# Two of four token tiles first: the first batch's hand-over from the second linear to the shared expert, split into halves

## The chip, the cores and the metric

The kernel runs on one core of a Trainium2 chip. The metric is device time in microseconds (us) of one execution. A profile records one execution, instruction by instruction; engines are named PE (TensorE), PEld (its weight loads), DVE (VectorE), ACT (ScalarE), POOL (GpSimd) and SP (SyncE).

## The reference

A gated cross-attention-like block on x of 4 batches x 512 tokens x 512 features, float32:

```python
# per batch b; smooth_quant_linear quantises tokens and weights to 8-bit steps after smoothing both per column
h = smooth_quant_linear(layernorm(x[b]), w_in[b])          # 512 -> 512
a = silu(h[:, :256]) * h[:, 256:]
x[b] += tanh(g_xattn) * smooth_quant_linear(a, w_ctx[b])   # the second linear, 256 -> 512
y = layernorm(x)                                           # all 2048 tokens
scores = softmax(y @ gate_w.T); top 2 of 16 experts, 256 places each
routed = sum over the two of weight * (silu(y @ wg[e]) * (y @ wu[e])) @ wd[e]
shared = (silu(y @ ws_gate) * (y @ ws_up)) @ ws_down       # inner size 704
out = x + tanh(g_ffn) * (routed + shared)
```

## The kernel before, in words

A batch is four tiles of 128 tokens on the partitions. For each batch, `first(b)` is the first linear (statistics, absolute maxima per column, smoothing, rounding, product) and `second(b)` the second one. For batch 0 the end of `second` is: `product(t)` (PE product into a bank of `ps_c`, then the DVE scale, L732), `residual(t)` (X += o, L739, on POOL unless told otherwise), `stats(t)` (DVE, L292 and L293), `norm` (one over the standard deviation of all four tiles, three steps of `inv_std`: L275, a square root on ACT at L266, then small DVE instructions L279 to L286), `normal(t)` (y, L753) and `turn_y(t)` (four PE transposes, L773, and an ACT copy, L354, into `xT`, features on partitions, tokens in columns).

The shared expert reads `xT`. `glu_steps` makes one chunk of 128 inner features: a gate product `pg` and an up product `pu` (L972), each four products over the features with 512 token columns (an f32 product is two passes, so it shows as two MATMULs), `silu` (L976) on ACT and `times` (L979) on DVE into `hT`. There are five full chunks, a rest of 64 features (`pr`), and then the products of tokens with ws_down (`sh`, L1037). These products are what PE fills its time with while the other engines work on the quantised linears of later batches.

Three things set the order on the engines. The **opening** (`Program`, L1250 to L1323) is an order written out by hand for batch 0 and the start of batch 1: `opening.at(time, steps)` sorts by time, the times being keys of the order alone. Its last block, `beside`, mixes products of shared chunk 0 with batch 1's maxima (`f1.greater`, `f1.turn_max`, `wide1`), smoothing, and its scaling of tokens (`divide`, DVE) and weights (`multiply`, POOL). `idle` and `idle_x` (L1266) are transposes whose results nobody reads. After the opening, a **Plan** (L1326) orders everything up to the routed experts by estimated durations, from given times at which each engine comes free; PE steps get a margin after what they need, and shared products (rank 1e6) fill the rest. From then on every engine runs its instructions in that order, each waiting for its semaphores. Last come the 16 **routed experts** (`gather`, `gate_up` L1154, `down` L987) and batch 3's shared products with the gathering of the results (`yk`, L1699).

PSUM is held in `ps_t` (tag tp, two banks), `ps_c` (tag c, two) and `ps_mm` (tag mm, four). `chain_ps` is the pair tp and c, `beside_ps` gives banks of `ps_mm`; `columns` (L299) takes the first of a pair for its transposes, `row_broadcast` (L307) the second.

## Time and profile before

| what | us |
|---|---|
| median of the three runs | 586.7 |
| lowest and highest | 576.94, 592.93 |
| the profiled execution | 580.96 |
| its span, first to last instruction | 579.0 |
| PE busy in the span | 538.2 |
| DVE busy | 406.4 |
| ACT, POOL busy | 228.0, 140.8 |

The profile gives, for each group or instruction, the start and duration in us, the line of the kernel, the operation, out<-in by the program's names with partitions x elements, and the count; in square brackets is how long the engine had stood idle before it and what ended that. A busy engine here means that an instruction was in flight; matmuls overlap, so PE's busy time is read together with the distances between starts. The granted clock is the share of full speed that TensorE was given.

### The profile page before, as it was taken

To read this page: it belongs to the slowest core of one execution; us is meant where nothing else is said; L and a number is where in the kernel's file an instruction comes from. 1 tells how busy PE (TensorE), PEld (TensorE's weight loads), DVE (VectorE), ACT (ScalarE), POOL (GpSimd) and SP (SyncE) were. 2 spreads that over 40 slices of the span, in tenths; PEclk is the share of its full clock that TensorE was granted. 3 is DMA by queue.
4 is the path that set the end of the run, shared out by engine and by line. 5 is a ranking of instruction groups with operands and counts; after the bars stand their busy time and mean duration, and the time that the engine had idled before them with its cause. 6 is when DMAs were issued, how large, how long until landed. Compare 5 with 4: busy or idle time off the path is not lost.

```text
span 579.0 us, 5971 instructions
## 1 busy us (share of the span) xinstructions
PE 538.2 (93%) x1830; PEld 283.9 (49%) x1830; DVE 406.4 (70%) x927; ACT 228.0 (39%) x379; POOL 140.8 (24%) x155
## 2 busy tenths in 40 slices
PE   0667799999999999999989999999999999999977
PEld 0544444544444444544455555555555555644422
DVE  6889788999998997985478666665755665315445
ACT  4554577538516353140146254444443444211000
POOL 1315032253261511201321022111111100027740
PEclk9978999999999999999999999999999999999989
DMA  8971012013205092010787999999999995336864
GB/s 283 366 243 37 1 73 72 1 44 82 57 1 109 15 326 68 2 72 3 169 253 219 219 284 282 250 269 271 291 241 261 287 259 144 86 101 199 247 216 164
DMA packets 93967, 95.07 MB, mean 164 GB/s; under 512 B 51552, under 2 KB 70240, under 8 KB 93936
## 3 DMA queue, kind: packets, MB, share of 16 engines
q1 hardware_dynamic: 84064, 69.39, 45.1%
q0 software_dynamic: 5120, 16.78, 9.2%
q10 hardware_dynamic: 4752, 8.52, 3.9%
q8 instruction: 15, 0.25, 0.2%
q14 instruction: 16, 0.13, 0.1%
HBM read 66.36 MB, written 16.78 MB: 144 GB/s over the span
## 4 chain that ended last, share of the span: by engine, by line
PE 75%; DVE 12%; issue 5%; POOL 3%; ACT 1%; DMA 1%; another core or an unknown queue 1%; SPq 0%; DVEq 0%; POOLq 0%
PE b L1154 22%; PE eo L987 14%; PE pg L972 9%; PE sh L1037 9%; PE pu L972 8%; POOL yk L1699 2%; PE pr L1011 2%; PE tp_h L1174 2%; PE acc L576 2%; DVE X L1710 1%; PE rowb L307 1%; PE sh L1043 1%; DVE scx L331 1%; PE acc L726 1%
## 5 line engine op out<-in xcount | busy, mean ns | idle before, releaser
L987 PE MATMUL eo<-wd,ehT 128*128 128x512 f32 (+1 forms) x192 | 85.1, 592 | 0.0
L1105 POOL DMA_INDIRECT xg<-xn_dram,slot_token x32 | 35.7, 1117 | 195.4 <-DMA xp<-xg 160.6
L1037 PE MATMUL sh<-wsd,hT 128*128 128x512 f32 x160 | 75.3, 607 | 4.0 <-DVE hT L979 4.0
L972 PE MATMUL pg<-xT,wsg 128*128 128x512 f32 x160 | 74.9, 597 | 0.7 <-ACT xT L354 0.7
L972 PE MATMUL pu<-xT,wsu 128*128 128x512 f32 x160 | 74.0, 595 | 0.0
L987 PEld LDWEIGHTS eo<-wd,ehT 128*128 128x128 f32 (+1 forms) x192 | 36.4, 190 | 41.6 <-issue 37.0
L354 ACT COPY xgT<-xp 128x1024 int16<-128x1024 int16 x31 | 39.5, 1339 | 27.6 <-DMA xp<-xg 27.6
L1203 DVE TENSOR_TENSOR p<-p,b 128x352 f32<-128x352 f32 x16 | 8.3, 520 | 57.6 <-PE b L1154 57.6
L1037 PEld LDWEIGHTS sh<-wsd,hT 128*128 128x128 f32 x160 | 29.5, 194 | 36.2 <-issue 30.5
L1699 POOL DMA_INDIRECT yk<-eo_dram,slot x32 | 32.6, 1020 | 51.5 <-PE pg L972 42.1
L972 PEld LDWEIGHTS pu<-xT,wsu 128*128 128x128 f32 x160 | 29.2, 190 | 30.8 <-issue 30.6
L972 PEld LDWEIGHTS pg<-xT,wsg 128*128 128x128 f32 x160 | 28.7, 190 | 31.0 <-issue 29.5
L1154 PE MATMUL b<-T,S 128*128 128x352 f32 x128 | 40.6, 460 | 0.7 <-DVE S L1145 0.7
L1154 PE MATMUL b<-wg,xgT 128*128 128x352 f32 x128 | 40.6, 460 | 0.0
L1154 PE MATMUL b<-wu,S 128*128 128x352 f32 x128 | 40.5, 459 | 0.0
L1165 ACT COPY eo_sb<-eo 128x512 f32<-128x512 f32 x32 | 18.7, 585 | 47.4 <-PE eo L987 39.4
L979 DVE TENSOR_TENSOR hT<-g,pu 128x512 f32<-128x512 f32 x20 | 13.6, 682 | 32.1 <-PE pu L972 15.6
L1154 PEld LDWEIGHTS b<-T,S 128*128 128x128 f32 x128 | 24.2, 190 | 14.5 <-issue 1.2
L1154 PEld LDWEIGHTS b<-wu,S 128*128 128x128 f32 x128 | 24.3, 190 | 13.5
L499 POOL TENSOR_TENSOR wi<-wi,s_row 128x512 f32<-128x512 f32 x16 | 19.9, 1272 | 42.5 <-ACT s_row L484 42.5
L1154 PEld LDWEIGHTS b<-wg,xgT 128*128 128x128 f32 x128 | 23.1, 190 | 10.9 <-issue 0.8
L1710 DVE SCALAR_TENSOR_TENSOR X<-yk,wk,X 128x512 f32<-128x512 f32 x32 | 23.4, 751 | 7.0 <-DMA yk<-eo_dram,slot 6.5
(235 smaller groups left out, 866.0 us busy)
## 6 DMA issues: line engine op xcount, KB each, us to landing
wg<-in_L_ffn_w_gate_dram SPq DMA_DIRECT2D x16, 704.0 KB, 7.7
wu<-in_L_ffn_w_up_dram SPq DMA_DIRECT2D x16, 704.0 KB, 6.3
wd<-in_L_ffn_w_down_dram SPq DMA_DIRECT2D x16, 512.0 KB
eo_dram<-eo_sb ACTq DMA_DIRECT2D x32, 256.0 KB, 2.0
X<-in_x_dram SPq DMA_DIRECT2D x16, 256.0 KB, 6.5
xn_dram<-yp SPq DMA_DIRECT2D x16, 256.0 KB, 2.0
out_dram<-X SPq DMA_DIRECT2D x15, 256.0 KB, 2.0
wi<-in_fside_BxS2xS_dram SPq DMA_DIRECT2D x3, 1024.0 KB
```

The lines of the kernel that those rows point to most:

```text
L354: return (vec.tensor_copy if on is vec else act.copy)(dst, src)
L499: on.tensor_tensor(w.wi[:, t, :], w.wi[:, t, :], v.s_row, ALU.mult)
L576: pe.matmul(accs[t], lhsT=block(b, w.xqT, k, t), rhs=block(b, w.wqT, k), start=(k == 0), stop=(k == HC - 1))
L972: pe.matmul(v.ps[name], lhsT=w[:, k, o : o + P], rhs=xT[:, k, :], start=(k == 0), stop=(k == HC - 1))
L979: vec.tensor_tensor(dst, v.g, v.ps["pu"], ALU.mult)
L987: pe.matmul(acc, lhsT=hT[:m, c, bass.ts(t, P)], rhs=wd[:m, c, :], start=(c == 0), stop=(c == len(chunks) - 1))
L1037: pe.matmul(accs[t], lhsT=s.hT[:, c, bass.ts(t, P)], rhs=wsd[:, c, :], start=(c == 0), stop=(c == last))
L1105: pool.indirect_dma_start(out=xg.rearrange("p l n -> p (l n)"), out_offset=None, in_=xn_dram, in_offset=bass.IndirectOffsetOnAxis(ap=slot_ ...
L1154: pe.matmul(ps[:, :I], lhsT=lhs[:, k, :], rhs=rhs[:, k, :], start=(first and k == 0), stop=(k == HALF - 1), skip_group_check=not first,)
L1165: act.copy(eo, R[e].acc[h])
L1699: pool.indirect_dma_start(out=yk, out_offset=None, in_=eo_dram, in_offset=bass.IndirectOffsetOnAxis(ap=slot[i % 2][:, tiles[i // 2] : tile ...
L1710: vec.scalar_tensor_tensor(X[:, j, :], yks[added[0]], wk[k][:, j : j + 1], X[:, j, :], ALU.mult, ALU.add)
```

## The change

The normalisation of batch 0 after the second linear, its transposes and the first shared products are split. Tiles 0 and 1 get their own inverse deviations (`norms[0]`), are normalised and transposed first; tiles 2 and 3 follow (`norms[1]`). Shared chunks 0 and 1 move into the opening together, and each of their products is issued in two halves of 256 token columns: three groups of first halves stand before the transposes of tiles 2 and 3, the fourth behind. residual(1) goes from POOL to DVE, scale(3) is issued apart from its product, and most idle transposes of that stretch are left out. `f1.turn_max` and batch 1's weight maxima take their bank from `ps_c`, as the four banks of `ps_mm` are held by the two chunks. In `beside`, both silus stand ahead of `row_s`, and both `times` at the end. The Plan starts with later times for PE, DVE, ACT and POOL and with shared chunks 2 to 4 of batch 0.

```diff
@@ -267,25 +267,30 @@
         else:
             pool.tensor_tensor(dst, src, power[:, : src.shape[1]], ALU.pow)
-    def inv_std(w, h, table=False):
+    def inv_std(w, h, table=False, ts=slice(0, TT)):
+        part = ts != slice(0, TT)
         def begin():
-            w.ve, w.r = small(TT, "ve" + h), small(TT, "r" + h)
-            vec.tensor_scalar(w.ve, w.mv[:, :, 1], LN_EPS, None, ALU.add)
+            if ts.start == 0:
+                w.ve, w.r = small(TT, "ve" + h), small(TT, "r" + h)
+            vec.tensor_scalar(w.ve[:, ts], w.mv[:, ts, 1], LN_EPS, None, ALU.add)
         def end():
+            r, ve = w.r[:, ts], w.ve[:, ts]
             if table:
-                vec.reciprocal(w.r, w.r)
-            c = small(TT, "c" + h)
-            vec.tensor_tensor(c, w.r, w.r, ALU.mult)
-            vec.scalar_tensor_tensor(c, c, -0.5, w.ve, ALU.mult, ALU.mult)
-            vec.scalar_tensor_tensor(w.r, c, 1.5, w.r, ALU.add, ALU.mult)
-            w.nmr = small(TT, "nmr" + h)
-            vec.scalar_tensor_tensor(w.nmr, w.mv[:, :, 0], -1.0, w.r, ALU.mult, ALU.mult)
-        return [begin, lambda: root(w.r, w.ve, neg_half, table), end]
+                vec.reciprocal(r, r)
+            c = small(TT, "c" + h)[:, ts]
+            vec.tensor_tensor(c, r, r, ALU.mult)
+            vec.scalar_tensor_tensor(c, c, -0.5, ve, ALU.mult, ALU.mult)
+            vec.scalar_tensor_tensor(r, c, 1.5, r, ALU.add, ALU.mult)
+            if not part:
+                w.nmr = small(TT, "nmr" + h)
+                vec.scalar_tensor_tensor(w.nmr, w.mv[:, :, 0], -1.0, w.r, ALU.mult, ALU.mult)
+        return [begin, lambda: root(w.r[:, ts], w.ve[:, ts], neg_half, table), end]
     def row_stats(mv, t, src, h):
         st = stat.tile([P, 6], F32, tag="bn" + h, name="bn" + h)
@@ -466,7 +471,7 @@
                 greater(t)
         def turn_max():
-            v.tp = columns(beside_ps if b == 1 else ps, v.am, HC)
+            v.tp = columns((ps[1],) if b == 1 else ps, v.am, HC)
         def column_max():
             v.ax = small(HC, "colx1")
@@ -805,6 +810,7 @@
         v.__dict__.update({k: f for k, f in locals().items() if callable(f)})
         v.smooth = smoothing(v, nk, "2", table=b == 0)
         v.norm = inv_std(v, "2", table=b == 0)
+        v.norms = [inv_std(v, "2", True, slice(2 * u, 2 * u + 2)) for u in range(TT // 2)]
         return v
@@ -960,16 +966,18 @@
             vec.tensor_tensor(wk[k], wk[k], den, ALU.mult)
-    def glu_steps(xT, o, dst, home):
+    def glu_steps(xT, o, dst, home, in_halves=False):
         pl, bufs = home
         v = SimpleNamespace(ps={})
-        def product(name, w, k):
-            if k == 0:
+        def product(name, w, k, ts=slice(0, S)):
+            if k == 0 and ts.start == 0:
                 v.ps[name] = ps_mm.tile([P, H], F32, tag="mm", name=name)
-            pe.matmul(v.ps[name], lhsT=w[:, k, o : o + P], rhs=xT[:, k, :], start=(k == 0), stop=(k == HC - 1))
+            pe.matmul(
+                v.ps[name][:, ts], lhsT=w[:, k, o : o + P], rhs=xT[:, k, ts], start=(k == 0), stop=(k == HC - 1)
+            )
         def silu():
             v.g = pl.tile([P, S], F32, tag="g", name="g", bufs=bufs)
@@ -978,6 +986,12 @@
         def times():
             vec.tensor_tensor(dst, v.g, v.ps["pu"], ALU.mult)
+        if in_halves:
+            halves = [slice(0, S // 2), slice(S // 2, S)]
+            gate = [[lambda k=k, ts=ts: product("pg", wsg, k, ts) for k in range(HC)] for ts in halves]
+            up = [[lambda k=k, ts=ts: product("pu", wsu, k, ts) for k in range(HC)] for ts in halves]
+            return gate, silu, up, times
         gate = [lambda k=k: product("pg", wsg, k) for k in range(HC)]
         up = [lambda k=k: product("pu", wsu, k) for k in range(HC)]
         return gate, silu, up, times
@@ -991,10 +1005,10 @@
     def shared(b, done=None):
         s = SimpleNamespace()
-        def chunk_steps(c, home=(shp, 2)):
+        def chunk_steps(c, home=(shp, 2), in_halves=False):
             if c == 0:
                 s.hT = shp.tile([P, len(CHUNKS_IS), S], F32, tag="hT", name="hT")
-            return glu_steps(xTs[b], c * P, s.hT[:, c, :], home)
+            return glu_steps(xTs[b], c * P, s.hT[:, c, :], home, in_halves)
         def chunk(c):
             gate, silu, up, times = chunk_steps(c)
@@ -1249,7 +1263,7 @@
     opening = Program()
     f0, (wide0, narrow0) = first(0), weights(0)
-    f1, (wide1, narrow1) = first(1), weights(1, beside_ps)
+    f1, (wide1, narrow1) = first(1), weights(1, (chain_ps[1],))
     s0 = second(0)
     def table(function):
         act.activation(small(1, "warm"), ones[:, :1], function)
@@ -1298,24 +1312,26 @@
     opening.at(46.7, *each(s0.steps_a), *each(s0.turn_a_tile), lambda: s0.take_a(act))
     opening.at(49.0, *each(s0.steps_w, vec), *each(s0.turn_w_tile), *f1.norm[:2], lambda: s0.take_w(vec), s0.row_ws)
     opening.at(51.2, f1.norm[2], *each(f1.absolute), lambda: s0.product(0), lambda: s0.product(1), lambda: s0.residual(0))
-    opening.at(53.5, lambda: s0.product(2), lambda: s0.residual(1), lambda: s0.stats(0), lambda: s0.product(3))
-    opening.at(55.0, lambda: s0.residual(3, vec), lambda: s0.residual(2), lambda: s0.stats(1), lambda: s0.stats(3))
-    opening.at(55.1, *each(idle_x, ts=[1, 2, 3]))
-    opening.at(58.0, lambda: s0.stats(2), s0.norm[0], *each(lambda t: idle(s0.mv[:, t, 0:1]), ts=[1, 3]), lambda: idle(s0.mv[:, 2, 0:1], 3), s0.norm[1], s0.norm[2], lambda: idle(s0.ve[:, :1], 3))
-    for t in range(TT):
-        opening.at(61.0 + 0.5 * t, lambda t=t: s0.normal(t, vec), lambda t=t: s0.turn_y(t))
+    opening.at(52.5, lambda: s0.residual(1, vec), lambda: idle_x(1), lambda: s0.stats(1), lambda: s0.stats(0), lambda: idle_x(0))
+    early, late = s0.norms
+    opening.at(55.0, early[0], early[1], lambda: s0.product(2), lambda: idle(s0.mv[:, 0, 0:1]), lambda: s0.residual(2), lambda: s0.multiplied(3), early[2])
+    for t in (0, 1):
+        opening.at(56.0, lambda t=t: s0.normal(t, vec), lambda t=t: s0.turn_y(t))
+    opening.at(57.0, lambda: s0.scale(3), lambda: s0.residual(3, vec), lambda: s0.stats(2), lambda: s0.stats(3), *late)
     sh0 = shared(0)
-    opening.at(64.0, *each(f1.greater, ts=[1, 2, 3]), *each(wide1.absolute), *each(wide1.greater, ts=[1, 2, 3]))
     def beside():
-        gate, silu, up, times = sh0.chunk_steps(0)
-        order = gate[:1] + [f1.turn_max] + gate[1:3] + [f1.column_max] + gate[3:] + [wide1.turn, wide1.end]
-        order += f1.smooth + [lambda: table(AF.Silu), silu]
-        order += up[:2] + [f1.row_rs, f1.row_s, *each(f1.multiply), *each(f1.divide)] + up[2:] + [times]
+        (gate0, silu0, up0, times0), (gate1, silu1, up1, times1) = (sh0.chunk_steps(c, in_halves=True) for c in range(2))
+        turns = [step for t in (2, 3) for step in (lambda t=t: s0.normal(t, vec), lambda t=t: s0.turn_y(t))]
+        order = gate0[0] + up0[0] + gate1[0] + turns + up1[0]
+        order += [*each(f1.greater, ts=[1, 2, 3]), f1.turn_max, *each(wide1.absolute), *each(wide1.greater, ts=[1, 2, 3])]
+        order += gate0[1] + [f1.column_max] + up0[1] + [wide1.turn, wide1.end] + gate1[1] + f1.smooth
+        order += [lambda: table(AF.Silu), silu0, silu1] + up1[1][:2] + [f1.row_rs, f1.row_s, *each(f1.multiply), *each(f1.divide)]
+        order += up1[1][2:] + [times0, times1]
         for step in order:
             step()
     opening.at(65.0, beside, lambda: s0.keep_normal(TT - 1), lambda: s0.store_normal(TT - 1))
     with tc.manual_schedule():
@@ -1324,7 +1340,7 @@
     plan = Plan(
-        dict(PE=74.5, DVE=76.5, ACT=74.0, POOL=78.0, SP=70.0, DMA=70.0, XBAR=70.0),
+        dict(PE=76.5, DVE=78.0, ACT=75.5, POOL=79.0, SP=70.0, DMA=70.0, XBAR=70.0),
         dict(tp=2, c=2, mm=4, h=3, ab=3, y=3, q=2, q2=2, aba=2, amx=1, amw=1, g=2, xT=2),
     )
     SHARED, ROUTE = 1e6, 1e5
@@ -1582,7 +1598,7 @@
     home0 = plan.add("ACT", 0.0, nothing, rank=-2.0, takes="xT")
     for t in range(TT - 1):
         plan_keep(s0, t, plan.add("ACT", 0.0, nothing, rank=-2.0, takes="y"), rank=KEEP)
-    plan_shared(0, sh0, [], range(1, FULL), home0)
+    plan_shared(0, sh0, [], range(2, FULL), home0)
     plan.margin = 3.0
     plan_scores(0, s0, [None] * TT)
     firsts, seconds = {0: SimpleNamespace(wi=None)}, {0: SimpleNamespace(wc=None)}
```

## The prediction, made before the changed kernel was run

> **What bounds the kernel now.** I read the page first, then the chain of waits, then the timelines of 48 to 90 us, where the change acts, and of 195 to 300 us, where its effect has to arrive.
>
> ```profile
> PE 538.2 (93%) x1830; PEld 283.9 (49%) x1830; DVE 406.4 (70%) x927; ACT 228.0 (39%) x379; POOL 140.8 (24%) x155
> ```
>
> TensorE is the bound: in windows of 10 us PE is busy throughout from 80 to 280 us, but for two holes of 0.7, and the chain gives it 75% of the span. The stretch where it is not full of real work is the head. PE's own timeline there:
>
> ```profile
> 53.98 0.66 PE L1266 MATMUL idle<-ident,X 128*128 128x128 f32 x4 [1.34 <-POOL X L739]
> 55.21 1.22 PE L1266 MATMUL idle<-ident,X 128*128 128x128 f32 x8 [0.58 <-POOL X L739]
> 56.58 2.61 PE L1266 MATMUL idle<-ident,mv 128*128 128x128 f32 x11
> 58.99 0.83 PE L1266 MATMUL idle<-ident,ve 128*128 128x128 f32 x3
> ...
> 63.22 1.12 PE L972 MATMUL pg<-xT,wsg 128*128 128x512 f32 x2 [0.68 <-ACT xT L354]
> ...
> 71.46 0.65 PE L307 MATMUL rowb<-ident,rs 128*128 128x128 f32 x4 [1.95 <-DVE rs L325]
> ...
> 75.19 3.27 PE L972 MATMUL pg<-xT,wsg 128*128 128x512 f32 x7
> ```
>
> The "idle" products are filler; real products begin at 63.22, behind the copy of the last tokens into xT, and PE waits once more, 1.95 us, for rs. From 75.19 on it never runs out. So whatever real work is done before 75 is saved at the end, as long as the other engines' chain keeps up. That chain is DVE's; its row that matters for the change is an add beside POOL's:
>
> ```profile
> 54.30 1.40 DVE L739 TENSOR_TENSOR X<-X,o 128x512 f32<-128x512 f32 x1
> ```
>
> **Part 1: the first half's path (earlier).** Durations are starts to starts in DVE's timeline: scale 0.72, statistics of one tile 0.80, a 4-wide instruction 0.20, a normal 0.46. Scale of tile 1 ends at 52.0. residual(1) moves from POOL to DVE and starts while POOL adds tile 0 (51.41 to 52.69). The row above is the nearest: a DVE add beside a POOL add took 1.40 and ended 0.55 after POOL's; alone such an instruction takes 0.69 (L461). So it ends at 53.25 (52.7 if nothing is shared; I take the first, the same pair of operations). Then stats(1), stats(0): 54.85; ve 55.2; scale(2) 0.75 covers the square root on ACT (0.20): 56.0; four small instructions: 56.8; normals 0 and 1 end at 57.4 and 57.9. Before, a tile took 0.6 in PE's transposes and 0.56 in ACT's copy; two tiles are in xT at 59.3. The first product starts at **59.4 instead of 63.2**.
>
> **Part 2: the second half's path (later).** Behind the early normals DVE has scale(3) 0.72, residual(3) 0.70, stats(2) and (3) 1.6, ve and root 0.6, four small ones 0.8, two normals 0.9: y of tile 3 at 63.3 instead of 61.38. The 1.9 us are the add taken from POOL (0.7), its wait for POOL (0.55) and the net four small instructions (0.8; five more, nmr gone), less waits that vanish. Queued behind them on DVE is f1.greater, batch 1's chain.
>
> **Part 3: half products.** 8 of 512 columns become 16 of 256 for each chunk. No 256-column fp32 row exists, but the neighbours agree on a price per column: 0.429 us a pass at 512 (L972), 0.296 at 352 (L1154), 0.109 at 128 (transposes): 0.84 ns. So a half product (two passes) is 0.43, its two halves cost what the whole cost. Each adds two weight loads: 32 for both chunks. *TensorE: Matmul & The Clock Gate* in the Trainium skill (Part 3, What overlaps and what doesn't) says that a weight load overlaps running matmuls only where the row groups differ, which these full-height products never do (its Part 2 also knows a background buffer that would allow it), and (LDWEIGHTS) prices a load at 128/1.2 = 107 ns: an estimate of 3.4 us more, nearly the whole gain. The rows speak otherwise: passes follow each other at 0.429 with a 0.19 us load each, and even transposes at 0.109 with a 0.14 us load. I take nothing; 3.4 stays as the bad end, below nothing is excluded as no work is left out.
>
> **Part 4: PE from 59.4.** In its order: 12 halves 5.15, transposes of tiles 2 and 3 0.87, 4 halves 1.72, turn_max 0.44, 8 halves 3.43, wide1.turn 0.44 (from 71.0), 4 halves 1.72, 2 halves 0.86: at 74.0 it stands before row_rs. y of tiles 2 and 3 (62.8, 63.3) are ready when PE comes to them at 64.5. The copies of xT end at 66.3, before the second-half products at 67.5.
> Row_rs needs rs: before, the reduce of wide1.end started 0.64 after the transposes and rs came 3.57 later; from 71.0 that is 75.2. PE waits 1.2. Then rowb 0.87 and 2 halves: **77.0**, with the score 78.0. Before, the score ran from 74.19, and it and chunk 1 would have ended at 75.19 + 6.86 = 82.05. **PE leads by 4.1 us.**
>
> **Part 5: the clock.** Filler is cut from 26 transposes to 12, so PE is nearly empty between 56.1 and 59.4 except for two transposed tiles (1.1 us).
>
> ```profile
> 52.85:56.27 3.42, 1.72 (x12) 1.00 0.00 0
> 56.27:59.68 3.41, 3.27 (x16) 0.50 0.00 0
> 59.68:63.10 3.42, 2.40 (x17) 1.00 0.00 0
> ...
> 69.90:73.30 3.40, 1.84 (x11) 1.00 0.00 0
> ```
>
> The columns are length, PE busy (instructions), granted clock, DMA share and GB/s; the cuts are the clock's own steps. A stretch with 1.72 of 3.42 us busy was followed by one at half clock; one with 1.84 was not. The same Trainium skill page (Why this matters for your kernels) warns only of gaps over some 3 us; after the change the gaps are 1.4 and 0.8 us, so by the rule nothing is lost and the lead is 4.1. By the rows, the new stretch from 56.27 has 1.4 us busy, under both, and the next 3.4 us, all half products, would run at half clock: 1.7 us lost, lead 2.4. The page (Part 1) also has the window free-running, so it need not fall there again; idle time enough lies inside for about half of its positions. I book 0.9, with ends 0 and 1.7.
>
> **Part 6: what comes late instead.** Wide1's maxima on ACT wait behind take_normal(2, 3), in one queue: from 63.06 to 66.2. Row_rs is 3.7 late; divides run from 75.9 (before 72.14). silu(0), silu(1) stand ahead of take_s on ACT, behind the 1.28 us table load: take_s 76.65 (72.58), POOL's multiplies end at 82.3 (78.2). times(0), times(1) stand ahead of max_x: 79.9.
>
> ```profile
> 75.38 2.28 DVE L331 TENSOR_REDUCE scx<-xn 128x4 f32<-128x2048 f32 x1
> 79.14 0.42 DVE L430 TENSOR_REDUCE rawc<-tp_am 128x2 f32<-128x256 f32 x1 [1.49 <-PE tp_am L299]
> ```
>
> So max_x is 4.5 late, but before there was a hole of 1.49 us behind it; scale_x is some 3 late. POOL's lateness is covered by that (max_w began at 81.64, 3.4 after the multiplies). The xn stores go to ACT and SP about 4 later; their readers, the gathers, start at 272.9. The c banks for turn_max and wide1.turn are free again before row_rs. The plan is told +1.5 for DVE and ACT, +2 for PE with one chunk less: it expects less lateness than I find, so a PE instruction of batch 1 will stand about 1 us waiting in order. I charge **1.0** (0 to 3).
>
> Is 3 us of lateness covered later? Batch 1's xT is complete at 135.2 while shared products last to 142.8; batch 2's at 206.9, to 218.0. At the end:
>
> ```profile
> 271.87 0.19 DVE L944 TENSOR_TENSOR slot_token<-slot_sum,st 128x32 int32<-128x32 f32 x1 [1.17 <-PE st L930]
> ...
> 280.85 1.33 ACT L354 COPY xgT<-xp 128x1024 int16<-128x1024 int16 x1 [16.76 <-DMA xp<-xg]
> ...
> 283.61 2.63 PE L1154 MATMUL b<-wg,xgT 128*128 128x352 f32 x8
> ```
>
> The first expert's tokens are ready at 282.2, 1.4 us before PE takes them. And in the last routing DVE stands waiting for PE's order four times (1.5 for tp_l, 0.5 for pu, 2.2 for pr through g_rest, 1.17 for st): 5.4 that shrink when PE is ahead. 3 late less 5.4 lets xgT come up to 2.4 earlier than before, about PE's lead. So it is covered.
>
> **The sum.** -4.1 + 0.9 + 1.0 = -2.2, say **-2 us**. The profiled execution took 580.96 (span 579.0 and 2.0 around it): 579. That execution is 5.7 below the median of the three runs; the middle of all four executions known is 583.8, so I forecast **582**.
>
> **Rivals.**
> - *The lead is given back.* PE stands in batch 1's chain until it is no longer ahead. For it: DVE is 80 to 95% busy from 80 to 250 us, so lateness is hardly made up. Against: 7.6 and 11 us of shared products remain behind each xT. Change 0: 584.
> - *Slower: batch 1's chain becomes the bound.* Place: take_s and max_x behind the silus and times. Price: 4.5 us at max_x, 6.2 with half clock. If the late order keeps DVE's waits for PE, it all reaches xgT, and the first expert starts 6.2 - 1.4 = 4.8 late: 588.5. It decides from the point where xgT is more than 1.4 later than 282.2. The plan that is off by 3 speaks for it; the four waits above against.
> - *It doesn't do what it says.* The head of the plan's block is already seen running inside the opening (batch 1's 128x256 maxima at 67.83, ahead of the root at 70.17), so order isn't only as written; were the first half's products to wait for all tiles (66.3), PE would have no lead: about +3, 587.
>
> **Chances.** -2 (from -5 to 0): 0.55; given back: 0.22; chain bound: 0.15; doesn't do it: 0.08. The runs of before spread over 576.9 to 592.9, 7 below and 9 above the middle, so 2% (11.7 us) is about what a measurement can tell from no change. Only the slow cases with a high draw pass +11.7, only the forecast with a low draw -11.7: 0.07 faster, 0.81 same, 0.12 slower. Range: 582 less 3 for the good end and 7 for the draw, 588 with 7, which also holds the weight loads' bad end (582 + 3.4): 572 to 595.
>
> **What would show it.** Right: the first L972 near 59.4 and at 0.215 a pass; an add of 1.2 to 1.4 on DVE at 52; rs near 75; max_x near 80; first b<-wg,xgT 1 to 4 us before 283.6. Wrong: passes over 0.25 (loads not hidden); PE waits of over 3 us in total between 80 and 280; xgT after 283.6.

## The result and the profile after

Slower. In six runs the changed kernel took 598.3 us (median; 592.7 to 605.3), the kernel before beside it 577.1: ratio 1.0351, 95% interval 1.0287 to 1.0414. The forecast was 582, no difference over 2%. The same kernel, measured again on two later occasions, took 587.8 against 576.0 (ratio 1.0198, 1.0171 to 1.0226) and 589.4 against 575.9 (1.0222, 1.0196 to 1.0249). In some sets of runs, that of the result among them, executions of either kernel are up to some 20 us longer by a wait in the last shared products, in others none is (the kernel before took 574.4 to 594.5 us in one set, 574.5 to 577.5 in another). So 12 to 13.5 us are the change's, and the other 8 to 9 of the 21 are put down to that wait.

The profiled execution took 599.9 us, span 597.7. The engine line of its page:

```profile
PE 542.2 (91%) x1844; PEld 292.6 (49%) x1848; DVE 410.0 (69%) x932; ACT 227.3 (38%) x380; POOL 139.5 (23%) x154
```

PE has 4 us more busy time and the span 18.7 more. PE's timeline where the change acts (start, duration, what, and in brackets the idle time before and what ended it):

```profile
53.22 1.80 PE L1280 MATMUL idle<-ident,X 128*128 128x128 f32 x8 [2.48 <-DVE X L744]
...
59.05 1.11 PE L778 MATMUL tp_x<-ident,y 128*128 128x128 f32 x8 [1.76 <-DVE y L758]
60.87 3.78 PE L978 MATMUL pg<-xT,wsg 128*128 128x256 f32 x8 [0.71 <-ACT xT L359]
64.45 3.21 PE L978 MATMUL pu<-xT,wsu 128*128 128x256 f32 x8
67.49 1.89 PE L978 MATMUL pg<-xT,wsg 128*128 128x256 f32 x8
69.22 1.04 PE L778 MATMUL tp_x<-ident,y 128*128 128x128 f32 x8
...
80.07 0.62 PE L312 MATMUL rowb<-ident,rs 128*128 128x128 f32 x4 [1.16 <-DVE rs L330]
...
81.92 1.06 PE L791 MATMUL logit<-xT,gateT 128*32 128x512 f32 x8
```

Real products begin at 60.87, 2.35 us earlier than before but 1.5 later than forecast. Eight half passes take 1.73 us at full clock (67.49 to 69.22), and the first eight 3.58. The transposes of tiles 2 and 3 have to wait for three such groups: 69.22, where the prediction had 64.5 for them. The score starts at 81.92 (74.19 before) and ends at 82.92. At that point PE has done the score and chunks 0 and 1, for which the prediction counted 82.05 in the kernel before: PE leaves the opening 0.9 us behind, not 4.1 ahead. The granted clock, cut at its own steps (length, PE busy, PEld, DVE, ACT, POOL, clock, DMA share, GB/s):

```profile
53.44:56.86 3.42, 3.42 (x15) 2.64 (x14) 2.48 (x8) 0.31 (x2) 0.12 (x1) 0.50 0.00 0
56.86:60.28 3.42, 1.54 (x10) 0.84 (x8) 3.28 (x7) 0.53 (x2) 1.15 (x1) 1.00 0.00 0
60.28:63.69 3.41, 2.82 (x7) 2.29 (x8) 2.92 (x10) 0.74 (x3) 0.00 (x0) 0.50 0.00 0
63.69:67.10 3.41, 3.41 (x10) 2.70 (x9) 2.99 (x5) 0.00 (x0) 0.00 (x0) 0.50 0.00 0
```

After the window with 1.54 us of PE work two windows run at half clock, not one. How many do differs between executions. In the profile of e_again the windows fall elsewhere: one from 58.58 to 61.98 holds 1.55 us of work, and only the one behind it runs at half clock. The first three groups of half products took 8.35 us here, 6.97 there and 7.71 in e_again2, against 5.19 at full clock. DVE's timeline:

```profile
51.95 1.21 DVE L744 TENSOR_TENSOR X<-X,o 128x512 f32<-128x512 f32 x1
...
55.91 0.75 DVE L737 SCALAR_TENSOR_TENSOR o<-acc,scx,ws_row 128x512 f32<-128x512 f32 x1 [0.81 <-PE acc L731]
...
56.77 1.25 DVE L286 TENSOR_TENSOR c<-r 128x2 f32<-128x2 f32 x1
...
72.01 2.28 DVE L422 TENSOR_TENSOR amw_w<-amw_w,ab_w 128x512 f32<-128x512 f32 x3 [5.24 <-ACT ab_w L418]
...
84.56 2.28 DVE L336 TENSOR_REDUCE scx<-xn 128x4 f32<-128x2048 f32 x1
```

DVE idles 5.24 us for the absolutes of wide1, which on ACT stand behind the copies of tiles 2 and 3; max_x, at 75.38 before, starts at 84.56. And the end, to be read against the lines of before (271.87 and 283.61):

```profile
284.49 0.19 DVE L950 TENSOR_TENSOR slot_token<-slot_sum,st 128x32 int32<-128x32 f32 x1 [1.78 <-PE st L936]
...
294.85 4.76 PE L1168 MATMUL b<-wg,xgT 128*128 128x352 f32 x8 [7.52 <-issue]
```

The 9.2 us of max_x have become 12.6 at the routing. PE runs out of shared products and stands 7.5 us, then starts the experts at half clock. Earlier its work came in another order: the second addition of batch 0's shared result (L1064) came at 138.7 instead of 143.7, but the first transposes of batch 1's y at 138.6 instead of 129.0, and between 140 and 160 PE was busy only 17.2 of 20 us (19.7 before). PE had done shared work early and stood later, when the chain was not ready. This is the order's doing and no lead of the opening: with the same opening and the order of before (e_order, below) that addition comes at 152.9.

Last, PE in the tail, where the result's execution stood (first two lines) and the first repetition, e_again, did not (third line):

```profile
562.42 2.74 PE L1051 MATMUL sh<-wsd,hT 128*128 128x512 f32 x6
574.18 6.99 PE L1051 MATMUL sh<-wsd,hT 128*128 128x512 f32 x10 [9.02 <-DVE hT L987]
```

```profile
563.31 7.03 PE L1051 MATMUL sh<-wsd,hT 128*128 128x512 f32 x16
```

### The profile page after: what moved, and what is told of

Same layout as the page of the kernel before. It is cut to its first block, busy times and chain, and to the rows that moved or that the text cites. A ratio compares the mean times of both kernels' runs of the same rounds, so it can differ in the third digit from the quotient of the medians.

```text
span 597.7 us, 6002 instructions
## 1 busy us (share of the span) xinstructions
PE 542.2 (91%) x1844; PEld 292.6 (49%) x1848; DVE 410.0 (69%) x932; ACT 227.3 (38%) x380; POOL 139.5 (23%) x154
## 4 chain that ended last, share of the span: by engine, by line
PE 81%; DVE 7%; DMA 6%; issue 2%; another core or an unknown queue 2%; SPq 1%; ACT 1%; POOL 0%; DVEq 0%
PE b L1168 22%; PE eo L1001 14%; PE sh L1051 12%; PE pu L978 11%; PE pg L978 11%; DMA wsu<-in_L_ffn_ws_up_dram 2%; PE pr L1025 2%; PE tp_h L1188 2%; PE acc L581 2%; PE sh L1057 1%; DMA X<-in_x_dram 1%; DMA wc<-in_ctx_dram 1%; PE acc L731 1%; DMA wg<-in_L_ffn_w_gate_dram 1%
## 5 line engine op out<-in xcount | busy, mean ns | idle before, releaser
L978 PE MATMUL pg<-xT,wsg 128*128 128x512 f32 (+1 forms) x176 | 76.0, 569 | 1.5 <-ACT xT L359 1.5
L978 PE MATMUL pu<-xT,wsu 128*128 128x512 f32 (+1 forms) x176 | 75.3, 564 | 0.0
L1168 PE MATMUL b<-wg,xgT 128*128 128x352 f32 x128 | 42.7, 479 | 7.5 <-issue 7.5
L978 PEld LDWEIGHTS pg<-xT,wsg 128*128 128x128 f32 x176 | 33.3, 196 | 31.3 <-issue 27.4
L978 PEld LDWEIGHTS pu<-xT,wsu 128*128 128x128 f32 x176 | 33.4, 196 | 29.9 <-issue 28.7
L1179 ACT COPY eo_sb<-eo 128x512 f32<-128x512 f32 x32 | 18.7, 585 | 49.5 <-PE eo L1001 41.5
L1168 PEld LDWEIGHTS b<-wu,S 128*128 128x128 f32 x128 | 24.3, 190 | 13.5
```

What stands on the lines that cost most here:

```text
L978: pe.matmul(v.ps[name][:, ts], lhsT=w[:, k, o : o + P], rhs=xT[:, k, ts], start=(k == 0), stop=(k == HC - 1))
L1168: pe.matmul(ps[:, :I], lhsT=lhs[:, k, :], rhs=rhs[:, k, :], start=(first and k == 0), stop=(k == HALF - 1), skip_group_check=not first,)
L1179: act.copy(eo, R[e].acc[h])
```

## The experiments

All differences in time below are against the kernel before, measured beside each version. Lateness is against the one profile of before at three places of batch 1's chain (the work of DVE, ACT and POOL on its linears, which PE's small products and transposes link): max_x of batch 1 (75.38), the first rounding of its tokens (xq, ACT, 80.68), which needs max_x, the batch's weight maxima and the sequence around batch 0's score, and the routing (slot_token, 271.87). The last column is the growth from xq to the routing. Such profiles differ by themselves: at 48 us, ahead of the change, they are between 0.5 us earlier and 1.1 later than that of before, and the three rows of the changed kernel differ by 1.3 us at max_x and 2.0 at the routing. Smaller differences in lateness say nothing; the growth is free of the shift at the start.

| kernel | order behind the opening | time - before | max_x | xq | routing | growth |
|---|---|---|---|---|---|---|
| changed, result's profile | new | +21.2 | 9.2 | 7.6 | 12.6 | 5.0 |
| changed, e_again | new | +11.8 | 8.5 | 6.9 | 12.7 | 5.8 |
| changed, e_again2 | new | +13.5 | 9.8 | 8.3 | 14.6 | 6.3 |
| e_clock | new | +8.5 | 5.6 | 4.0 | 8.9 | 4.9 |
| e_turns | new | +10.9 | 5.3 | 6.9 | 11.8 | 4.9 |
| e_chain | new | +6.5 | 0.5 | 2.6 | 7.5 | 4.9 |
| e_plan | planned from other times | +17.1 | 9.4 | 9.7 | 17.5 | 7.8 |
| e_start | planned from other times | +15.7 | 5.6 | 4.1 | 15.1 | 11.0 |
| e_delay | that of before | +9.8 | 9.9 | 8.3 | 9.3 | 1.0 |
| e_lead | that of before | -4.1 | 0.0 | -1.5 | -3.4 | -1.9 |
| e_order | that of before | +8.9 | 9.5 | 7.9 | 9.8 | 1.9 |
| e_both | that of before | -1.4 | 0.1 | -0.3 | 0.7 | 1.0 |

**Lateness of the chain alone.**

```diff
-        order += up[:2] + [f1.row_rs, ..., *each(f1.divide)] + up[2:] + [times]
+        order += up[:2] + [f1.row_rs, ..., *each(f1.divide)] + up[2:] + [times] + [lambda: row_max(f1.xn, "x1")] * 4
```

> The kernel before, with nothing of the change in it, but four more reduces of xn (2.28 us each on DVE in the profile of before, 9.1 us together; their results are not used) stand ahead of max_x of batch 1. The change made max_x 9.2 us late; this makes it late by the same without touching PE's work. Theory A (lateness of batch 1's chain is never made up and arrives at the first expert): the routing is 8 to 12 us late and the time is 8 to 13 us above before. Theory B (the prediction's: lateness is covered by slack, the loss has another cause, such as the clock or the halves): routing less than 4 us late, time at most 4 us above before.

585.6 against 575.9: ratio 1.0169 (1.0148 to 1.019).

```profile
76.50 11.05 DVE L331 TENSOR_REDUCE scx<-xn 128x4 f32<-128x2048 f32 x5
...
281.12 0.19 DVE L944 TENSOR_TENSOR slot_token<-slot_sum,st 128x32 int32<-128x32 f32 x1 [1.17 <-PE st L930]
...
292.87 2.63 PE L1154 MATMUL b<-wg,xgT 128*128 128x352 f32 x8
```

Theory A holds. max_x, the last of the five, is 9.9 us late: 8.8 by the four reduces, and 1.1 because PE, at half clock from 72.5 to 75.9 in this execution, finished the up product later. At xq 8.3 are left (before had a hole of 1.49 behind max_x), and at the routing it is 9.3; the transposes of y and the scores of batches 1 to 3 in between are 8.6 to 9.3 late. Nothing is made up in 200 us. PE, whose work was not touched, is late by the same at the first expert: it waits in its order for the chain (5.12 us for xq at 89.76).

**A lead of PE alone.**

```diff
-            pe.matmul(v.ps[name], lhsT=w[:, k, o : o + P], rhs=xT[:, k, :], ...)
+            ts = slice(0, 64) if o == P and k and not SHORT else slice(0, S)
+            pe.matmul(v.ps[name][:, ts], lhsT=w[:, k, o : o + P], rhs=xT[:, k, ts], ...)
...                                     # SHORT is filled behind batch 0's chunk 1: later batches are whole
```

> The kernel before, in its own order, with less PE work and nothing else: six of the eight products of batch 0's shared chunk 1 run over 64 token columns instead of 512, which leaves out part of that chunk's result. A column took 0.84 ns a pass, two passes each: 6 x 448 x 2 x 0.84 ns = 4.5 us less PE work, just where the change takes its own from. Theory P (the prediction's: PE is the bound from 75 us on, so a lead of PE is kept to the end): 4 to 4.5 us faster. Theory A (the chain of the other engines sets the routing; a lead turns into idle PE): within 1 us of before, and PE idle 4 us more before the first expert.

572.0 against 576.0: ratio 0.9933 (0.9911 to 0.9956).

```profile
268.44 0.19 DVE L944 TENSOR_TENSOR slot_token<-slot_sum,st 128x32 int32<-128x32 f32 x1 [1.17 <-PE st L930]
```

The prediction's theory holds here, and A's "a lead turns into idle PE" falls: some 4.5 us less work gave 3.4 at the routing and 4.1 in time. But it came at least in part through the chain: max_w of batch 1, which in before stands behind PE's turns of batch 0's score, was already 2.2 us earlier at 79.4. PE and the chain wait for each other in an order fixed beforehand. A delay of the chain was passed on whole (e_delay); a lead of PE helped where the chain stands behind PE.

**Half clock.**

```diff
-    ... lambda: s0.residual(1, vec), lambda: idle_x(1), ...
+    ... lambda: s0.residual(1, vec), *[lambda: idle(s0.xs[:, :1])] * 5, lambda: idle_x(1), ...
-    ... lambda: s0.multiplied(3), early[2])
+    ... lambda: s0.multiplied(3), *[lambda: idle(s0.ve[:, :1])] * 3, early[2])
+    opening.at(56.5, lambda: idle(s0.ys[1]))
```

> The changed kernel with 40 idle transposes put where PE stood empty between 50.9 and 60.9 us (20 behind the third product, 12 ahead of the y transposes of tiles 0 and 1, 4 behind these), so that the clock should stay full. Half clock cost 3.2 us of PE between 60.9 and 69.2 and some 1.0 in the second linear. Theory A (chain bound): the transposes of tiles 2 and 3 come 3 to 4 us earlier, max_x too, and the time falls by 3 to 5 us from that of the changed kernel. Theory C (half clock is the whole loss, as PE is the bound): PE's work is 4 us earlier and the time falls to that of before or lower, 15 us and more. Theory D (the loss is in the order that the plan makes): nothing beyond 1 us.

584.4 against 575.9: ratio 1.0148 (1.0128 to 1.0168). The same windows:

```profile
56.86:60.28 3.42, 2.45 (x21) 1.94 (x19) 3.28 (x8) 1.07 (x2) 0.59 (x1) 1.00 0.00 0
60.28:63.69 3.41, 3.37 (x16) 2.99 (x17) 2.90 (x12) 0.20 (x1) 0.00 (x0) 1.00 0.00 0
63.69:67.10 3.41, 3.41 (x21) 3.08 (x20) 2.46 (x5) 0.86 (x2) 0.00 (x0) 1.00 0.02 5
```

With 2.45 instead of 1.54 us of work in the window the clock stays full. The price of half clock is 3.3 us against e_again (8.5 for 11.8) and 5.0 against e_again2 (13.5), near what theory A had, and not the whole loss. Of the lateness at max_x 5.6 are left.

**The order in the opening.**

```diff
-        order = gate0[0] + up0[0] + gate1[0] + turns + up1[0]
-        order += [*each(f1.greater, ...), f1.turn_max, *each(wide1.absolute), *each(wide1.greater, ...)]
-        order += gate0[1] + [f1.column_max] + up0[1] + [wide1.turn, wide1.end] + gate1[1] + f1.smooth
-        order += [lambda: table(AF.Silu), silu0, silu1] + up1[1][:2] + [f1.row_rs, ...]
-        order += up1[1][2:] + [times0, times1]
+        order = gate0[0] + turns + up0[0] + gate1[0]
+        order += [*each(f1.greater, ...), f1.turn_max, *each(wide1.absolute), *each(wide1.greater, ...)]
+        order += up1[0] + [f1.column_max, wide1.turn, wide1.end] + gate0[1] + gate1[1] + f1.smooth
+        order += [lambda: table(AF.Silu), silu0, silu1, f1.row_rs, ...]
+        order += up0[1] + up1[1] + [times0, times1]
```

> The changed kernel with another order in the opening's last block: the normals and transposes of tiles 2 and 3 stand behind one group of half products instead of three, wide1's transposes behind two groups less, and row_rs ahead of the last two groups. PE's work is the same in amount. Theory A: rs near 76 instead of 79.7, max_x near 80.6 instead of 84.6, so 4 us less lateness in the chain, and the time falls by 4 us (3 to 6) from that of the changed kernel. Theory B (lateness is covered): no change beyond 1 us, or slower by what PE waits more.

586.8 against 575.9 (1.0162 to 1.0205 as a ratio). max_x came 4 us earlier, at 80.64, as expected, but the time fell by 1 only against e_again (2.6 against e_again2): the last two groups now stand behind row_rs on PE, so the score started at 81.19, 0.7 before that of the changed kernel, and batch 1's first rounding was again 6.9 us late. max_x is one of two links there; PE's score and the turns behind it are the other.

**The plan's start times.** They were set to what the profile has.

```diff
-        dict(PE=76.5, DVE=78.0, ACT=75.5, POOL=79.0, ...),
+        dict(PE=82.0, DVE=84.5, ACT=82.0, POOL=87.0, ...),
```

> The changed kernel with the plan's start times as its profile has them: PE 82.0, DVE 84.5, ACT 82.0, POOL 87.0 instead of 76.5, 78.0, 75.5, 79.0. The opening is untouched. Theory A (the opening makes the chain late): the time stays within 3 us of the changed kernel. Theory D (the plan's order, made for an opening that ends 6 to 8 us earlier, makes or keeps the lateness): 5 us or more faster than the changed kernel, with max_x as late as in it but the routing less late.

593.0 against 575.9: 17.1 us above before, where the changed kernel was 11.8 and 13.5. Neither theory had this: with max_x as late as in the changed kernel, the routing was 17.5 late. The last column of the table tells why. Growth is 4.9 to 6.3 with the changed kernel's order, whatever the opening does, 1.0 in e_delay with the order of before, and 7.8 here. So the order itself seems to have a price; e_order and e_both below test it. The next run took the start times of before instead, with the filler of e_clock:

> The changed kernel with the 40 idle transposes of the experiment on the clock, and the plan's start times of before (PE 74.5, DVE 76.5, ACT 74.0, POOL 78.0) instead of the changed ones. Between max_x of batch 1 and the routing the lateness grew from 5.6 to 8.9 us with the changed ones, while in the kernel before with four dummy reduces it grew by 1 only. Theory D (the plan's order adds the growth): another order, so another growth, the time differs from 584.4 by more than 2 us in either direction. Theory A alone: 583 to 586.

591.8 against 576.0: growth 11.0. Better or worse start times do not tell a good order from a bad one.

**The chain put back.** Besides e_clock's filler:

```diff
-    ... lambda: s0.residual(2), lambda: s0.multiplied(3), ...
+    ... lambda: s0.multiplied(3), ...
-    opening.at(57.0, lambda: s0.scale(3), ...
+    opening.at(57.0, lambda: s0.residual(2, vec), lambda: s0.scale(3), ...
+        order = gate0[0] + up0[0] + each(s0.normal, vec, ts=[2, 3])
+        order += [*each(f1.greater, ...), *each(wide1.absolute), *each(wide1.greater, ...), *each(s0.turn_y, ts=[2, 3])]
+        order += gate1[0] + [f1.turn_max] + up1[0] + [f1.column_max, wide1.turn, wide1.end] + gate0[1] + up0[1] + f1.smooth
+        order += [lambda: table(AF.Silu), silu0, f1.row_rs, f1.row_s, ..., *gate1[1], silu1, *up1[1]]
+        f1.products = [times0, times1]
-        n = add("DVE", 2.35, f.max_x, *over, rank=r + 8)
+        n = add("DVE", 2.35, lambda: [step() for step in (f.max_x, *f.products)], *over, rank=r + 8)
```

> The changed kernel with the idle transposes, and with the chain put back ahead: residual(2) on DVE behind the first two normals, normals of tiles 2 and 3 behind two groups of half products, wide1's absolutes on ACT ahead of the copies of tiles 2 and 3, wide1's transposes ahead of the second halves, row_s ahead of silu(1), and both times behind max_x. PE's first product still near 59.5 and both chunks done near 77.5, so PE leads by some 4 us. max_x is expected at 75 to 77 (75.4 before). Theory A (chain sets the end): the routing is 0 to 4 us late, the time within 4 us of before in spite of PE's lead. Theory P (PE's lead counts): 3 to 4 us faster than before.

582.5 against 576.0: ratio 1.0115 (1.0088 to 1.0142).

```profile
75.89 2.29 DVE L336 TENSOR_REDUCE scx<-xn 128x4 f32<-128x2048 f32 x1
...
279.36 0.19 DVE L950 TENSOR_TENSOR slot_token<-slot_sum,st 128x32 int32<-128x32 f32 x1 [1.79 <-PE st L936]
```

max_x started at 75.89, xq was 2.6 late: on PE the transposes of the weight maxima (tp_am), which DVE needs for it, stood behind six passes of chunk 2 and came at 80.59, where e_both below, with the same opening, has them at 77.51 and xq on time. The routing was still 7.5 late. Theory A alone falls: an opening on time is not enough.

**The old order behind it.** The plan is made as before; chunk 1's steps do nothing.

```diff
-        dict(PE=76.5, DVE=78.0, ACT=75.5, POOL=79.0, ...),
+        dict(PE=74.5, DVE=76.5, ACT=74.0, POOL=78.0, ...),
-    plan_shared(0, sh0, [], range(2, FULL), home0)
+    plan_shared(0, sh0, [], range(1, FULL), home0)
-                steps.all = s.chunk_steps(c)
+                steps.all = ([nothing] * HC, nothing, [nothing] * HC, nothing) if b == 0 and c == 1 else s.chunk_steps(c)
```

On the changed kernel's opening:

> The changed kernel's opening, with the instructions behind it in exactly the order of before on every engine (the plan is made as before, start times and chunk 1 included, and chunk 1's steps, already done, do nothing). In the kernel before, 8.3 us of lateness at max_x stayed 9.3 with that order, and 4.5 us less PE work gave 3.4 at the routing. Theory D (two parts: what the opening makes late, and an order behind it that adds to it): max_x again 8.5 to 9 us late, the routing 5 to 9 late instead of 12.7, the time 581 to 585 against 587.8 of the changed kernel. Theory A alone (the opening's lateness is the whole): no change beyond 1 us.

584.8 against 575.9: ratio 1.014 (1.0119 to 1.0162).

```profile
84.90 2.28 DVE L336 TENSOR_REDUCE scx<-xn 128x4 f32<-128x2048 f32 x1
...
281.69 0.19 DVE L950 TENSOR_TENSOR slot_token<-slot_sum,st 128x32 int32<-128x32 f32 x1 [1.17 <-PE st L936]
```

9.5 late at max_x, 7.9 at xq, 9.8 at the routing: most of the growth is gone, and with it 4.6 of the 13.5 us of the changed kernel beside it. And on the opening with the chain put back:

> The kernel with the chain put back ahead in the opening (idle transposes, wide1's maxima early, both times behind max_x), and the order of before behind it. There max_x was 0.5 us late and the routing 7.5. Theory D: with the old order the lateness does not grow, and PE's lead of some 4 us shortens the chain's waits as it did with less PE work: the routing 2 to 3 us earlier than before and the time 2 to 3 us below before. Theory A alone (the order is not the cause of the growth): the routing again 7 us late, 582.

574.6 against 575.9: ratio 0.9973 (0.9963 to 0.9983), the one complete version measured below both kernels, by 1.4 us.

```profile
58.89 2.00 PE L978 MATMUL pg<-xT,wsg 128*128 128x256 f32 x8 [0.29 <-ACT xT L359]
...
81.20 0.61 PE L366 MATMUL tp_q<-ident_h,xq 128*128 128x128 bf16 x4 [2.21 <-ACT xq L356]
81.61 2.02 PE L978 MATMUL pg<-xT,wsg 128*128 128x512 f32 x2
...
272.61 0.19 DVE L950 TENSOR_TENSOR slot_token<-slot_sum,st 128x32 int32<-128x32 f32 x1 [1.17 <-PE st L936]
```

The same opening differs by 8 us with the two orders (e_chain +6.5, e_both -1.4). Products begin at 58.89, 4.3 us before those of the kernel before, and both chunks are done at 76.5. With the score and the small transposes behind it PE is at 78.8 where it stood at 82.8 before: the forecast lead of 4 us is there, and the chain is on time, but only 1.4 us of it arrive. What becomes of the lead is in the lines: where chunk 1 stood in the order, PE waits 2.21 us for xq, and behind the wait two passes of 512 columns take 2.02 us instead of 1.08, half clock again. What the new order adds up to xq is the place of tp_am told at e_chain; why it adds some 4 us more from there to the routing was not traced.

**Where the lead is lost.** Twenty idle transposes in that hole:

```diff
-            o = add("PE", 0.0, f.open_x, steps[0], ...)
+            o = add("PE", 0.0, lambda: [step() for step in (*f.filler, f.open_x)], steps[0], ...)
+        f1.filler = [lambda: idle(s0.xs[:, :1])] * 5
```

> The last kernel (chain ahead in the opening, order of before behind it: 574.6 us) with 20 idle transposes on PE ahead of the transposes of xq, where chunk 1 stood in the order of before. There PE now waits 2.2 us for xq, and its clock was 0.83 over the next 20 us, 3 us of PE lost. If PE's lead was lost in this hole and the half clock behind it: the routing 2 to 3 us earlier, 571.5 to 573.5 us. If the lead does not matter there: within 0.7 us of 574.6.

```profile
78.94 2.35 PE L1280 MATMUL idle<-ident,scx 128*128 128x128 f32 x20
...
81.56 1.08 PE L978 MATMUL pg<-xT,wsg 128*128 128x512 f32 x2
...
270.86 0.19 DVE L950 TENSOR_TENSOR slot_token<-slot_sum,st 128x32 int32<-128x32 f32 x1 [1.17 <-PE st L936]
```

Full clock behind it, and the routing 1.0 us before that of before and 1.75 before e_both's. The three other profiles of this order (e_fill2, e_fill3, e_best) have the routing 1.3, 0.2 and 0.0 us before that of before; the growth from xq, free of the shift at the start, is -0.4 to -0.9 in all four against 1.0 in e_both. So 1.4 to 1.9 us of the lead had been lost in the hole and the half clock behind it. Whether that reaches the end isn't settled. These runs had the wait in the tail (580.9 to 593.2 against 575.6 to 594.3, ratio 0.9993 to 1.0231), and so had two repetitions, the first of which is

> The kernel with 20 idle transposes in chunk 1's place, once more: its first timing fell among executions with the wait of hT, 580.9 to 593.2 us, though its routing came 1.0 us before that of the kernel before and 1.75 before that of the one without the filler. Without the wait: 572 to 574 us, 2 to 3.5 below before. With it, 575 to 593 again, like before beside it.

with 574.3 to 593.6 against 574.4 to 594.5 (0.9971 to 1.0069). The last, e_fill3, gave 574.2 to 594.4 against 574.5 to 595.1 (0.9976 to 1.0087):

> The kernel with 20 idle transposes in chunk 1's place, a last time. In its two profiles the routing came 1.0 and 1.3 us before that of the kernel before (0.7 behind it without the filler); the times so far spread over 574 to 593 us as those of before beside them, by the wait of hT. Without that wait: 572 to 574 us if the 1.75 us at the routing reach the end, 574.6 if the end has another bound. With the wait nothing new.

The lowest of 50 runs is 574.2, the lowest of before beside them 574.4: no gain over e_both is shown. The other way to close the hole moves chunks 2 to 4 of batch 0 up by one place:

> The same kernel (574.6 us) with batch 0's shared chunks 2, 3 and 4 each moved one place up in the order of before, chunk 2 where chunk 1 stood, so that the empty place is that of chunk 4, some 20 us later. Theory: PE stays busy at full clock between 79 and 88 us, but the waits of batch 1's chain for PE are those of before plus the 2.3 us by which the first score is late, until the empty place comes, where the chain gains what PE no longer has to do: the routing 1 us late to 2 us early, 573 to 577 us. If the lead is simply added wherever the empty place is: 571 to 573.

Neither: the routing was 4.3 us late, 0.7 of it from the first instructions on (ratio 1.0017 to 1.0272, with the same wait about). With chunk 2 at chunk 1's place PE was again between the chain and its turns: max_w came at 84.90, 3.3 late, and chunk 4's empty place, 20 us on, gave nothing back. In this pair of runs the place of the missing work decided what the lead was worth.

**The wait in the tail.** In the result's profile hT on DVE stood 9.56 us, and in those of e_fill and e_shift 10.1 and 10.2, until POOL's gathers of the results (yk) were over. The changed kernel was run again, twice, and once with another operation for hT:

```diff
-            vec.tensor_tensor(dst, v.g, v.ps["pu"], ALU.mult)
+            vec.scalar_tensor_tensor(dst, v.g, 1.0, v.ps["pu"], ALU.mult, ALU.mult)     # batch 3
```

> The changed kernel itself, unaltered, beside the other kernels of this call. In its profile the experts end 12.5 us later than before and the last products of tokens stand still for 9.0 us for hT, a wait that none of the first four experiments showed. If that wait belongs to the change, the time is again 593 to 605 us. If it comes from where the gathers of the results fall in an execution, it can be absent: then the lateness of the chain alone is left, 12.6 us, and the time is 586 to 590.

> The changed kernel, unaltered, once more, to set the next kernel against. It took 598.3 us in the result and 587.8 in an experiment. The difference lay in the last shared products, where hT (a TENSOR_TENSOR on DVE) stood 9.0 us until the gathers of the results on POOL were over. With that wait 593 to 605 us, without it 586 to 590.

> The changed kernel with batch 3's hT computed by SCALAR_TENSOR_TENSOR (g times 1.0 times pu) instead of TENSOR_TENSOR. In the opening a TENSOR_TENSOR of two columns took 1.25 us beside a POOL add, and SCALAR_TENSOR_TENSORs ran beside POOL work at their usual 0.7. If hT in the tail is held up by POOL's gathers because of its operation, the wait is gone in this kernel: 586 to 590 us whatever the unaltered kernel of the same call takes. If hT waits for something else, both kernels take the same time. If the unaltered kernel has no such wait here, this says nothing.

587.8, 589.4 and 587.2: the changed kernel without the wait, twice, which gives the change's own price; for the operation nothing was told. Made in the kernel before, with the rest of hT too, it was run where the wait was about:

> The kernel before with batch 3's hT (chunks and rest) computed by SCALAR_TENSOR_TENSOR (g times 1.0 times the up product) instead of TENSOR_TENSOR; nothing else. In some executions of before and of the changed kernel hT stands 4 to 10 us until the gathers on POOL are over, and the times then spread over 576 to 605 us. If TENSOR_TENSOR is what POOL's gathers hold up, this kernel takes 575 to 577 in every run, wherever before spreads. If the wait has another cause, this kernel spreads as before does. Where before shows no spread in this call, both take 576 and nothing is told.

574.7 to 595.0 against 574.4 to 594.5, ratio 0.9983 to 1.0103: it spreads as before does, and its profile has the wait with the other operation:

```profile
560.99 0.69 DVE L980 SCALAR_TENSOR_TENSOR hT<-g,pu 128x512 f32<-128x512 f32 x1 [26.88 <-remote]
```

The operation is not the cause, and ACT stood 16.9 us there too (g_rest), so it isn't DVE's alone. The version with filler and this edit together took 581.7 to 593.9 beside it, no better:

> The same kernel with batch 3's hT by SCALAR_TENSOR_TENSOR as well. If TENSOR_TENSOR is what the gathers hold up: 572 to 574 us in every run, with or without the wait in the kernels beside it. If not: as the kernel without this edit.

What holds the engines there stays open; that the wait is not the change's is shown by the kernel before, whose profile has it (hT at 561.2 behind 7.7 us of standing) and 31 of whose 43 runs beside e_tail2 took 579.9 us and more. The experiments without the wait ran on chips 4 and 6, those with it on chips 13, 1 and 7 (the result's isn't recorded); whether the chip decides is not shown.

## Why the prediction was wrong

- **What bounds the kernel.** The prediction had TensorE as the bound and work done before 75 saved at the end, "as long as the other engines' chain keeps up". e_lead supports the first half (4.1 of 4.5 us, in part through the chain), e_both only in part (1.4 of some 4, with the chain on time). The failing part was the condition: the chain did not keep up.
- **Part 1**, 59.4: measured 60.87. The add ended where it was put (53.16 against 53.25). Not seen were scale(2), whose product stood on PE behind idle transposes that waited for residual(1) and ran at half clock (0.81 of waiting), and residual(2) on POOL, which held a two-column TENSOR_TENSOR for 1.25 us instead of 0.16. With both gone and the clock full (e_both) the first product is at 58.89.
- **Part 2**, y of tile 3 at 63.3: 64.6, by the same 1.3 to 1.5.
- **Part 3** held. A half pass took 0.216 us (1.73 for eight), so weight loads cost nothing; the 3.4 us worked out from the page did not appear.
- **Part 5**, 0.9 for the clock: 3.2 (8.35 us for the first three groups, for 5.19 at full clock). The stretch did fall to half, and for two windows, past the bad end of 1.7. The trace's rows were nearer than the page's gap rule; the half odds that I gave them and the single window were the error. In e_again, with one window, it was 1.8.
- **Part 4**: score end 78.0 forecast, 82.9 measured; 1.5 and 3.2 make 4.7 of the 4.9. With it the forecast lead of PE is gone: -0.9 against 82.05, not 4.1.
- **Part 6** first half: max_x forecast 79.9, measured 84.56. The same 4.7. So the opening's order was followed correctly and two terms, the start of the products and the clock, were mis-sized.
- **Part 6** second half failed outright, and it is the step that turned a gain into a loss. "Covered" rested on slack at xgT and four waits for PE's order in the last routing. e_delay shows that 8.3 us of lateness at xq arrive as 9.3. The waits stay, as PE, in its fixed order, becomes late with the chain: the last one, for st, is 1.17 in e_delay as before.
- **The plan's order** was charged 1.0 for start times that were off. It cost 4.6 us of time between e_again2 and e_order, and 7.9 between e_chain and e_both; from xq to the routing lateness grew by 4.9 to 6.3 with it, by 1.0 to 1.9 with the order of before (e_delay, e_both, e_order). The plan with one chunk less made another order altogether. The sum, from the first repetition: 6.9 late at xq, 5.8 more to the routing, 12.7 there, 11.8 in time.
- **The base.** I took the middle of four executions, 583.8; before without the tail's wait takes 576. Its profile showed that wait (3.97 us on PE at 561.95, for hT), and the prediction did not ask whether it belonged to every execution. The result's 598.3 contains more of it (PE stood 9.02), which is why it lies above the range: without it the kernel took 587.8 and 589.4.
- **Rivals.** "Batch 1's chain becomes the bound" is what happened, with 12.7 us of lateness at the routing for its 6.2. Its 588.5 is close to the two repetitions, but by luck: two errors cancel, a price less than half as large (4.8 for 11.8 to 13.5) and a base 8 too high.

## What to carry to other kernels

In an order fixed beforehand, engines that wait for each other can pass on a delay whole, as 8.3 us became 9.3 here; count slack only where a trace shows idle time that doesn't itself come from that order. When a block of work leaves a planner's input, the new order may have a price of its own, 4.6 and 7.9 us here: keep the old order with an empty place to separate the two. Filler on PE can be worth more than it costs when it keeps the clock full, and a lead that opens a hole can be lost in it and in the half clock behind it, as in e_both.

## What the runs showed of the hardware

- A window of 3.42 us with 1.54 us of PE work was followed by one at half clock, and that one, with 2.82 us of work, by a second; with 2.45 us in the first there was none. A half-clock window with 2.93 us of work (e_both, 80.70 to 84.13) was also followed by a second, one with 3.27 (before, 56.27 to 59.68) was not. The amount alone does not settle whether a first one comes: 1.72 us (before, 52.85 to 56.27) was followed by one, 1.64 in e_tail (51.95 to 55.36, counted back from the clock's step at 58.78) was not. *TensorE: Matmul & The Clock Gate* in the Trainium skill (Why this matters for your kernels) warns only of gaps over some 3 us; here no gap was longer than 1.76 in that window.
- A TENSOR_TENSOR of two columns took 1.25 us on DVE beside a POOL add of 512 columns, and 0.16 without it (e_both, 55.74), while scale, with one input in PSUM, ran at its usual 0.72 inside POOL's adds (before, 53.55). *GPSIMD Engine Reference* in the Trainium skill (Specifications) names DVE instructions with two SBUF inputs among those that contend with POOL, and these rows agree. What was paid did not go by size: the two columns ended at 58.02, just behind POOL's add (58.00), and the DVE add of 512 columns at 53.16, 0.55 behind POOL's (52.61).
- In the profiles of before, of the changed kernel, of e_fill and of e_shift DVE stands 7.7 to 10.2 us for hT in the last shared products, in those of e_fill3, e_tail2 and e_best 26.8 to 26.9, while POOL issues its gathers back to back (one in 1.25 us), and goes on 1.3 to 5.5 us behind the last of them. In the other profiles with the same instructions it doesn't. No experiment here found the cause.
